# GpSimd's long instructions wait for their turn on the port that they share with VectorE, in a kernel whose order is written out ahead

## Chip, cores, metric

One core of a Trainium2 chip. The metric is the device time of one execution in microseconds, the median of the runs. In the profile PE is TensorE, PEld its weight loads, DVE VectorE, ACT ScalarE, POOL GpSimd and SP SyncE, whose queue issues most of the transfers.

## The reference

128 graphs of 64 nodes with 256 features pass through four layers, each added to its input and then normalised (layer norm):

```python
# layer 0: a gated graph network, five steps l
m = h @ weight[l]; agg = A.T @ m          # A = (adj != 0), per graph
r = sigmoid(agg @ Wir + h @ Whr + b); z = sigmoid(agg @ Wiz + h @ Whz + b)
n = tanh(agg @ Win + b + r * (h @ Whn + b)); h = (1 - z) * n + z * h
# layer 1: y = silu(rmsnorm(((adj + eps*I) @ x) @ W1 + b1) * w) @ W2 + b2
# layer 2: y = expmap0(adj @ logmap0(x)), projected onto the unit ball
# layer 3: attention by exp(e_i + f_j + b) over the neighbours
```

All of it is float32.

## The kernel before

Two graphs make a block of 128 rows and four blocks a group: 16 groups of 512 rows. `group(g)` writes a group's work: `gated` for the five steps of layer 0 (tiles hT, agg, tA, tB, U, V, hnb, banks p_ga, p_gb, p_gc, p_hx, p_hy, p_ix, p_iy), then layer 1 (aggm, ts, hid, sqt, sqh, xb, banks p_ah, p_bh, p_ch, p_ox, p_oy), layers 2 and 3 (tan, hw, x3T, banks ps_sup, ps_a, ps_att). Matrix products are cut into halves and combined by sums, in the manner of Strassen and Winograd, so that seven products do for eight. The sums of inputs are VectorE additions of two SBUF tiles (`sums`, line 445 in the profile: tA, tB, ts, s). The last two groups use simpler forms, and the last one is cut into pieces.

Nothing is issued where it is written. `flow.op(engine, us, run, writes, reads, ...)` records an operation with a planner's estimate `us` of its time and, for transfers, `kb`, a size that the planner uses. Work of several groups is open at a time. A search that is no part of the kernel made the string `ORDER`: each sign names the engine, the group and the place of the operation that is issued next. `Flow.placed` decodes it and `Flow.issue` calls each operation; on an engine each instruction is ordered behind the one before (`BEHIND`, which costs no semaphore). Between engines only true data dependencies hold an instruction back. So each engine follows its own list, and how two engines' lists run beside each other is decided on the chip.

An operation carries `port` where it uses the SBUF port that VectorE and GpSimd share: all GpSimd operations (`pool`, `few`, `few_s`, `pool_sum`, `w2_less`), and on VectorE those with two SBUF inputs (`summing`, `times_state`) or copies and scalings within SBUF. Before the change only the search used this mark.

GpSimd's longer work, with the profile's mean of one: additions of 128x512 in layer 1 (sqt, line 448: 1.3 us), additions of 128x1024 for biases (xb, x_n, line 448: 2.4 us), powers of a few numbers for norms (rstd line 845, inv line 1260, few lines 1151, 1323, 1341, 1345: 1.0 to 1.7 us), and at the start the sums of weights (w_a, w_in line 536; w2f line 681: 0.5 to 1.4 us). Its short operations (few, mv, ve, lines 438 and 442) take 0.2 to 0.3 us.

Row and feature layouts are exchanged by VectorE transposes of 32x32 squares (tile t, line 888 and 1366) and four SBUF transfers per tile on SyncE's queue (`moved`, line 790: hr from t, and x3T from t).

Of the kernel before, what the change touches and what calls it, by code (L numbers as in the profile page):

```python
# [53 lines left out]
class Flow:  # L54

    ENGINES, AHEAD = ("PE", "DVE", "ACT", "POOL", "SP"), 6
    SIGNS = "ABCDEFGHIJKLMNOPQRSTUVWXYZabcdefghijklmnopqrstuvwxyz0123456789!#$%&()*+,-./:;<=>"
    ORDER = ("CEEg~PhD~BNhED~BOiDC~Bs$CAAAAAAAAAAAAAAAAii~Nr~Nr~BO~N.~CU8~B+88~Bt~Bt8$~Bt~BL~Bt88li~BL~FU~FU~FU~FU"
             "~BL!i~Et~BL~Bt!~FZ~Bs~BL~FZ~BpEe~Bt~D%~BL~EO~BLA~DAi~DAB~DA~BoB~Bo~CUBF~BogiFFF~B+~B+HG~B+~GiAA~BK8~"
             "GjEC%~DB%B~BO%~FZAB~C3~BL~Es~E:~B<EA%B~CUlB~Et~BsB~CZBE~C5AB~CaE~BV~B+~C0~DiF,FA~D$H$~CBA~DE~CW~BsA~"  # L60
             "EQA$~BM~EQC&Ag~Dx~DBC~CV~DK~GK~Bs~CVgF&&~DxC~DGF%H~BsfBEF9(~EdA~B:AEj(jBB~Dx~D8~D8~MDAA~CJjkEBjFk~Mh"
             "x(~DA~Np~DAAx~MD~MDGl~BKT~NL~CJAH~DB~BdEA>CBAxe~Bdh~MBC~Lze~BpC~B+~Br!~BNxTA8TCG8~CB~CB~BN8B~J9!9DAD"
             "eAgDACCFB~CXCAAhBh~D8AKA~DABKK~DKKL~By~Do~BNLhFF~BV~BV#K~CAH#~G#PKhP~DA~Ce~B0~DA~Bt~DBKD~CAK~B0~BtPM"
             "~CAA~BV~By~IVA,P+CB8uh~BKA8A~Bp~Bq+gAC~BN~BNF;~BN~FZ~BNFBFBFuD~D%HFD~BQFKDGK~DjM~DF~Bu~BtL~Bt~Bt&M~B"
             "tMFHpFHFk%Fko&ooGoFqFGlopA(GpAlpH~BQA~BygG~CyoC&Ao&CoC~BQhAqGAG8Ag~BrBKGDKMA*DKgnKCh~DFnMDAPJBAKRDfK"
             "BD+B+B+~Bt~BQ~BQ~BQB+~JjEE~EP~D%E~BvpE~I3BK~BQB~BoA~DA~BqAA~BKA~B+~BoC~BM9~CUAA~BV~BVAAACBBC~Bo~Bo~B"
             "Veee!AC9FC~GAf~GAB8~CVABeGAg~EoC~Eo~BL~Bo(~BpA(AAAAB~CyAAKBKKAL!~BtA!kAA~BtCFCFBFFBFHFfHGKAAB~FeBKgK"
             "&CKkGKBMKKBKLBKK-~CA~CAKLM~ByM~ByMK~BU-KM~Bz~ByLK~BU~BVLKpKMKFBMFBKKBKMBKKBKK~BLEKE~BL~Ce~BL~Ce~Eo~C"
             "eEGEGLlL~DA~DA,,FKGKHKL~Bo~BoA~BqAAAG-~BoGC~BoK-9AG~BMAAGCAGAAB!88GC8ACBeeBgAfAC8B8B8BAGAGAC~Eo~BQJC"
             "*~EonA~BQ~BLAJA~BQAABAAAABAA~BMA!AfCACFF9FFBFHeBFfAFBFAgFBHFCKFBFBKqKGMFBHF~B:~B:H,~DALHo~B:L~B:~B:G"  # L70
             "F~BRp~CaKH~B;KFpH~BPBFBM~Bt~BtB%%LFBMBjlj~Bol~Buij~BLij~BL~BP~BLijEG%GL%jj~D8L~BQ~Cy~Bo&~DAFL~BR~H+L"
             "~BRF~H+L~BqF~BLHAALAA~B+~CBC~Bo~BqL~BMA~CUALAC~BVOA~BVAOB8ABsCeOB8CeGAgAfCB~GAF~GA8BA~CVAB~E+CA~BpjC"
             "kAA88AAABA~HUjBF~Bo!9A!AAlAHFGgeCGKKBKKKBMKfAGABFBg+G~CACK~BWBooBKBKM~Ce~BLoKB-~By~Byp~By~B0L~By~CeB"
             "q~CeMKB~HUMBKK~BziFE~BzFp~BUE~BL~BUE~EoL-oGop~Boq~CAp~CA~BL~CyGK~BLlK~BzM~Bo~BLFKG~DeHK~BLAAG~DAAG~B"
             "-A8CG~BoKG~BM8GAAG8CeAGfeBeeeeBg~BuACAgf8C8B~GAB~GAB8~B,AGAA~BQnC~Eo~BQJC~EoLAJ~BLAJ~BpAAABAAAABAA!A"
             "!FeCFFFCFHBF%BFfAABFBEgFGFCjBj(FB~B:~B:~B:BF~BtB(~Bt~Bt~BvGBjHAKHABAAoo~BpKBKLAAAAKG~BW~B:FBMB~BtBM~"
             "G%H~Bu~G%MFDG~BP~BMLF!~BQKgKGkHFCF~CaGFH~EtLDDHKLF~BQKDLCFK9gLFLCFqFDGFKFLFMFGAAFL~BRAACL(FALAALA8CL"
             "AeBA~D8BC8L8f~DAgpAA~CULCF~BVs~DKlAOBHA~BVsFG~BoOABAk~DKGABj~BV~By!kFg~ByFGDl~DKG~BV~DKAH~BVB~DK~DK~"
             "B0KGKK~B0KGC~By~CekM~ByC~CA,D+,~ByC~By~BU~B0B+~BWG~BV&KKMD~By~By~By~By~BWL8KqMAAGKGpCpAKCAAGK~BQAM*B"
             "LAJ~E:BK~BQKgAJ~BQJABCD~Bt~Bt~D%DC~CZ~IZDC~IZ~BQK~BQFFDFFK~CZH%~BvLFAAAAFBDFHFFGAA(AA~C3BH~BP~BPH~BP"  # L80
             "B~BPFlfKKB%~G%Gg+9j!B+KCBoHo~F*~FJ~E7~E7B!KK&gFLA!AA&ACAGKGCFApA-KGA~Bp-AjpqjBMAAlKBAF~Bu~EtLH~BtpA~"
             "Bt~BLoL~BtpFBKF~BL%LFfq~B:kKFL~BtfMA~D8~D8G~D8AAL(AAAL(AAApAFLAF,AAA9AAfFFL~ByfAHLAHAL~B+~B+~B+~B+~B"
             "Q~BY~B+A~BV~BysA~BKGs~CejkO~D+~BVA&AA~BVAAf~I8G~CefFB~BMF!~IeGGl~DKA~BVAH~FAK~BV~Ey~Ey~BQ~EyK~C!AGK~"
             "CeGK~CC~ByMkAAAG~BWAKG~JK~BU~CfK~CfKK,M~HyGo~BzoL-oKGqKMLnK~BQAnKMB~BdKLgK~BdKM~BQTK~BQCKT~BVKDLx!K>"
             "K!~CenCK~BzxCKLDKJDKD-T~BtK-~EPqKhhM~Bt~ErphoL~CZD~CZLh!~DFDpgDK~BQ~E:~BQFFgLKC~BaDFD~GjqDLF;DM~DjDD"
             "~B:D~FZHL~Bt~Bv~C3L~C3~BRF~Ca~E$~Bt~BP~E$~CaF~E$~CaCFDGDF~B:&DDCjGgjLgjAC~BQjLe~BRLeA~BML%g%Gg~CBjC~"
             "EPp~BRDFFL(FsDDFks~FA~BV~EyslF~BVHO~CZCG%~B:D&FDD&DF~BPGFDDF&(BF(~By9j~E$fH~ByBHKK~B0G~FAKKDG~EU~BM~"
             "Ce~BVFk!~D+~BVM~D++GC+C~CAl~C9F~C9KJ~BUGDK~C9HK~C9K~BWG~IeMDDKp~IALoLqoGM~BU~BUCGoCpogoGKqGGKMKCKKMB"
             "~Bt~BtoBKD~BVEKLEK~BuKEELFFFFFFKk~BWKKG-KGKMGKMIlp~E3(,P~C%LHoLp~C%PHKLPKII~CUqLPO~CUM~BoI~BRuAL~BKl"
             "eHL~CjpeHA!LFFCfIFFgfgeCe9CA~B,HABBBFRF999FF~BLBFHfjFB~E:H>~E:DgGKTKKFG!T%CGL%TFCFLl~D%D~BzH~D%D%~C5"  # L90
             "G%DFB!FkCKPGCKPPPlEGAAgF~CUBMD~CUFC~EUFGAAGCDGKCKIBMAA~BU+pC(H-AfADB~C8~C8KApoppAgDgDpKC~ByLH~DK~DK~"
             "CBCDKM~IACLK+L+DHMKL~GoKAAA,,A+pB+-ID~CfKLKM~By~ByLIAAAA~B,9IKKlBHH+HKK~CefFBFF9IBFHFFFF~CAFFH~BMBH!"
             "FGFG~D%G~D%%~BV%GCFF~Bqk~CZCL~CZ!%G%CBKFFkCKKGKf(~BtBl~BV~Bt~BuKFIMFMLoHAAMf9AAAAHALeHeeILA~BtHpK~BL"
             "MKGIAALLFFqfAAMAAf%HALAAALFFLAALeA~FALAA9AALA~DKfA~DKp~ByLeAAAf/A~DoG/~Bo~BoGs~Bo~BoFBO(AA~BVl888~BV"
             "AAIABFB~IeH~ByIHAAA~BzA~BMAIA~Bz!AABKHxK~EU~BVK~B7CKI~Do~Bd~DoLC~Do~By~B7~CgKD,T~BMK~C9K!>o~C9MTK~Cf"
             "FCTpFFLFoGKpMI~HyMCLoKpFF~CfhMFFkKDD&KlKKMDKD!KM~Ey#kklK~EyG~BUKKHDDhDK~C1DG~CBHKKkLHDDDDKDDHGKlKL!K"
             "GKGMKoM~DFpFqL~C3MLHFpFFKLKqL~Bt~Bt~BtG~Bt~BtM~Bt~BtFLFLFFLLL~By~By!~CeLp~DoDDDCDC~CeFL!8~B;C~DK/Asg"
             "sC~CZeOA~CZgCCkkkFFFCFF~BVF~BV~BVGkDFFFFFkFkF~B0F~CZ~CZDD~Ba~BV~CZ~DK~BV~DKGCF~DK~B0~BVD~DKDDDD~BV~D"
             "KKK;~B0KKM~By~By~By~ByKD9Bf~BWKMB~Ce~CeD~BMK,,oKL!KCKKCpKMDMKDMD~FAM~FA!LKKCBC+KK~C8BB~BOLKK,DKK$EL-"
             "EKKpKqKF~Bt,MLFoM~BP~BPL~BPpKKL~BPFFFLqk~BoMG~BoF~BRL88L(8L!~BM!L8LAAC~Fs~ByCFCLF~E$FFCFFCpFLAeOG/l~"  # L100
             "BVA~EyAOH~BVfO~C8BBIl~ByBYBl9~DPfYB~EZ~Ce~BEBl~DPBHfmBIDxC~BV~D:x~DKgI~IA~IA~BVKCKTK~BVKC~ByLIT~ByID"
             "~C8~Bil,D2KH,KYlDKILYgmKIY~BUm!LK~COKgLoLoCKI,IM~B$EKKDFDHGD~GjDkKKFML~DKk~DKD~CfKDKD;KKgFDM;DFDDk+g"
             "f+H,~C8~C8!~C8,~C8K~BVK~Cg,K~DKGMKL~BU--~BU~Bzo~BzK~BzM~BUp~BU~BuML~BUB~F8-poo~CBKp~ByM~ByB~ByKKKKKL"
             "~By~ByLKp~BWKK-KKq%,MFLoFLFpHKKLFLqFFMG~C3~BV8~BPL~BP~B:,8,F~BMA!LA,gFCL~BPjjLDlFH~BY~Bu~EyD&~DKC/D~"
             "DKGs~By~BV~ByOlGjH~DKGDDkDFDFGG~IADD~IAH~BV~BVK~BVKK~BVK~ByHM~ByG~BW~C8G+K~BW+kBKGKMpKLoooKG~BWKM~BV"
             "~BtM~G+KMLp+pGk~F8+KKqfM~EyGB~Bt*~CZKB*LD~BMKJ~BVJK~BQCKCKKKCKL~D%~BQ~Dj~BQDDL-DfKpKKK~BQ-~CZ~BQFMFF"
             "FKC~Bt~BtH9C~BQCFj,~B:MBj~BRFLEjHFiLo&i~BtDGEKpHjjLHjKGq~BtkFlL~BPH~G%G~GjMFG%G%LFlLF~BuH~EtL~Et~BV~"
             "BtA~BQ~Bt~Bu~BtLFLF%LFFkAG~B:CAC~BzF(~BzF~BzA(LFFOCAHs~BKHeOGCAOG9eCkACffFfCfACB~ByBFGAlJG~ByBBH~CeB"
             "f~CeB~DKG>K~B0KKTGK~ByMD~Do,~Dok~ByxCT~DKKkCok~BW~CeoCGKCK~BuMD~C8DK-L+~BW+Dq~ByLCF~BVFoMF~BVFMFFF,F"
             "KCG+Ck+CKG~E3EB~E:DG~BM~E:GCF~Et~B;KCk~C8CDKK~BuKH~Byp~EtDMF~BuDKKfCF~EPfFCDjFAGAAACFF~BVFA~BVAAGAF~"  # L110
             "BVCFAeAB(B(ACBFBAAAACAFClAAAHB8ABAGgAgAGkFCDAGC8FlD8GKC~BLK+CD~ByL~BoHBA~BWKGAGKC8GMAfAKB+KGg~CAKLgD"
             "~By~ByL-~ByA&MDA~BWKB~BUM~CeGMKg~Bz~HyC+~BzKLD~BUL~BU~BUGo-KGDKM*~EyM~ByLJ~EUJ~BzKLAJA~BVAA~BQ~BUKB~"
             "BQKDKKLK~Bt~BQLAAAA~EPB-~EPK~Bp~BvK-~EP~BQf~Bt~BvKBKKM9~D%MB~D%~Bv~CZL~CZ~DFLFFLFCFBKHK~BQCL%L%gF&FB"
             "qKHFLAGFM~BP~BPHLFHFLFH%G~GjH%gG~GFACG%G~F3CLFFBg~CUFHfAAHBFCA~BQA8AfAFLFF~BpAfAAAfAFfAAAGAAALAAeLFF"
             "pFeLeFGOAFOf~BRFfFs(~BVAAOAHkFHBAAA&AABAAGAAGeAAAA~BVBjF~BVkGAAAAlF~E7~FJB~E7~ByGA!AAHAAAA!GA~By~CnB"
             "KKGCTKK+CGx~CAMxD~BQ+g>~ByG+g>GKCxKGCKT~CAGMD~CAD~CAD~CA-LJ~CA~CCKJLq~C8~BtLJo~CBM~CB~CeJD~BUDD!K~Ba"
# [1326 lines left out]
```

## Time and profile before

| | |
|---|---|
| median of 3 runs | 2286.3 us (2285.16 to 2289.82) |
| the profiled execution: time, span | 2287.12 us, 2284.7 us |
| TensorE, weight loads, VectorE busy | 98%, 87%, 80% |
| ScalarE, GpSimd busy | 57%, 23% |
| granted TensorE clock | 0.994 |
| chain that ended last: TensorE, VectorE, DMA | 92%, 4%, 2% |

Busy time of TensorE is counted from the start to the modelled end of each matmul. Matmuls overlap, so a busy TensorE may still issue them more slowly than it could; the distance from one start to the next tells that. Every float32 matmul appears as two records. A duration on VectorE or GpSimd includes the time in which the instruction was blocked after its start.

### The profile page before, as it was taken

Reading aid. Unit: us, or ns where it says so; the run is one execution under the profiler, and the core shown is the slowest. Engines: PE = TensorE matmul, PEld = TensorE weight load, DVE = VectorE, ACT = ScalarE, POOL = GpSimd, SP = SyncE. Lnnn points to the kernel's source line nnn. Section 1 sums busy time; section 2 is a strip of 40 time slices with the busy share of each in tenths; the row PEclk is TensorE's granted clock in tenths of the full one; section 3 lists DMA queues with packets and bytes.
Section 4 is the critical chain, followed back from the end, with each engine's and each line's share of the span. In section 5 each row is a group of like instructions: output and inputs, shape, how many; then the busy total and the mean of one; then the engine's idle time right before and its main releaser. Section 6 shows DMA issues by size and latency. Waiting matters only on the chain.

```text
span 2284.7 us, 34183 instructions
## 1 busy us (share of the span) xinstructions
PE 2239.7 (98%) x12050; PEld 1983.1 (87%) x12050; DVE 1827.2 (80%) x3846; ACT 1304.0 (57%) x2842; POOL 533.6 (23%) x827
## 2 busy tenths in 40 slices
PE   8999999999999999999999999999999999999987
PEld 6888898888888898988989889898988989888875
DVE  6687788887887878888778887888788788877886
ACT  2444556665555656556565656656566565654565
POOL 4100213332213212132231212222122231210222
PEclk9999999999999999999999999999999999999998
DMA  5022112112212122121212212112221212211100
GB/s 155 15 29 37 22 28 59 19 22 47 56 15 45 37 31 56 22 40 28 35 40 36 51 22 39 39 29 47 31 37 29 40 38 35 42 29 19 33 20 28
DMA packets 430042, 84.58 MB, mean 37 GB/s; under 512 B 399236, under 2 KB 428960, under 8 KB 429872
## 3 DMA queue, kind: packets, MB, share of 16 engines
q1 hardware_dynamic: 428144, 80.52, 19.8%
q8 instruction: 95, 1.56, 0.3%
q10 hardware_dynamic: 1328, 1.31, 0.2%
q0 software_dynamic: 400, 0.57, 0.1%
q14 instruction: 75, 0.61, 0.1%
HBM read 32.55 MB, written 8.39 MB: 18 GB/s over the span
## 4 chain that ended last, share of the span: by engine, by line
PE 92%; DVE 4%; DMA 2%; SPq 1%; ACT 1%; issue 1%; POOL 0%; POOLq 0%; DVEq 0%; ACTq 0%
PE p_ga L926 23%; PE p_gc L926 11%; PE ps_agg L399 7%; PE p_ix L932 6%; PE p_hx L932 6%; PE p_gb L926 6%; PE p_ah L1109 5%; PE p_iy L932 4%; PE p_ox L1184 4%; PE p_hy L932 4%; PE p_oy L1184 3%; PE p_ch L1109 2%; PE ps_a L399 2%; PE ps_wmih L399 1%; PE ps_sup L399 1%; DMA hr<-t 1%
## 5 line engine op out<-in xcount | busy, mean ns | idle before, releaser
L442 POOL TENSOR_SCALAR mv<-st 128x4 f32<-128x4 f32 x56 | 16.3, 292 | 767.5 <-ACT x_n L828 422.6
L926 PE MATMUL p_ga<-hT,w_h 128*128 128x256 f32 x640 | 177.7, 380 | 1.1 <-DVE hT L1051 1.0
L926 PE MATMUL p_gc<-tA,w_h 128*128 128x256 f32 x640 | 178.5, 380 | 0.1
L926 PE MATMUL p_ga<-tA,w_h 128*128 128x256 f32 x640 | 177.7, 381 | 0.0
L926 PE MATMUL p_gc<-tB,w_a 128*128 128x256 f32 x640 | 175.7, 380 | 0.7 <-DVE tB L445 0.7
L926 PE MATMUL p_ga<-agg,w_a 128*128 128x256 f32 x640 | 173.3, 380 | 0.3 <-DVE agg L426 0.3
L926 PE MATMUL p_ga<-tB,w_a 128*128 128x256 f32 x640 | 171.8, 379 | 0.0
L399 PEld LDWEIGHTS ps_agg<-edge,hr 128*128 128x128 f32 x1024 | 148.3, 191 | 17.4 <-issue 2.8
L399 PE MATMUL ps_agg<-edge,hr 128*128 128x128 f32 x1024 | 152.4, 276 | 3.2 <-DMA hr<-t 3.2
L979 ACT ACTIVATE U<-U,half_b 128x512 f32<-128x512 f32 (+1 forms) x160 | 95.1, 629 | 91.2 <-DVE U L976 91.2
L430 ACT ACTIVATE hnb<-p_hx,half_b 128x256 f32<-128x256 f32 x197 | 92.6, 471 | 92.0 <-PE p_hx L932 74.5
L926 PEld LDWEIGHTS p_ga<-tB,w_a 128*128 128x128 f32 x640 | 120.3, 190 | 16.4 <-DVE tB L445 0.3
L926 PEld LDWEIGHTS p_gc<-tB,w_a 128*128 128x128 f32 x640 | 119.7, 190 | 17.0 <-DVE tB L445 1.3
L926 PEld LDWEIGHTS p_gc<-tA,w_h 128*128 128x128 f32 x640 | 118.7, 190 | 16.0 <-DVE U L992 0.5
L926 PEld LDWEIGHTS p_ga<-agg,w_a 128*128 128x128 f32 x640 | 118.2, 190 | 16.1 <-DVE agg L426 1.2
L926 PEld LDWEIGHTS p_ga<-hT,w_h 128*128 128x128 f32 x640 | 117.2, 190 | 16.1 <-DVE hT L1051 1.2
L926 PEld LDWEIGHTS p_ga<-tA,w_h 128*128 128x128 f32 x640 | 116.8, 191 | 15.8 <-ACT U L425 1.5
L979 ACT ACTIVATE V<-V,half_b 128x256 f32<-128x256 f32 (+1 forms) x160 | 89.1, 587 | 69.2 <-DVE V L976 68.7
L845 POOL TENSOR_TENSOR rstd<-ve,pow 128x4 f32<-128x4 f32 (+2 forms) x67 | 79.8, 1191 | 137.0 <-DVE ve L843 128.3
L992 DVE TENSOR_TENSOR V<-p_ix,V 128x256 f32<-128x256 f32 x192 | 80.6, 421 | 34.6 <-PE p_ix L932 30.3
L425 ACT COPY agg<-ps_agg 128x512 f32<-128x512 f32 x131 | 76.2, 583 | 47.2 <-PE ps_agg L399 45.8
L1184 PE MATMUL p_oy<-w2f,hid 128*128 128x128 f32 x720 | 101.1, 278 | 0.5 <-ACT hid L1160 0.4
(289 smaller groups left out, 6152.5 us busy)
## 6 DMA issues: line engine op xcount, KB each, us to landing
hr<-t SPq DMA_DIRECT2D x256, 128.0 KB, 3.8
x<-in_x_dram SPq DMA_DIRECT2D x64, 128.0 KB, 2.6
xr<-in_x_dram SPq DMA_DIRECT2D x16, 512.0 KB, 3.4
xs<-in_x_dram SPq DMA_DIRECT2D x120, 64.0 KB, 2.4
out_dram<-x_n SPq DMA_DIRECT2D x15, 512.0 KB, 2.9
x3T<-t SPq DMA_DIRECT2D x56, 128.0 KB, 3.8
edge<-in_adj_dram SPq DMA_DIRECT2D x64, 32.0 KB, 2.3
wm<-in_L_gnn_weight_dram SPq DMA_DIRECT2D x5, 256.0 KB, 3.8
```

The source lines that it names most:

```text
L399: return nc.tensor.matmul(o, lhsT, rhs, start=(k == 0), stop=(k == nk - 1))
L425: flow.either([("ACT", on_act(n, r), lambda: nc.scalar.copy(o(), i())), ("DVE", 0.145 + 0.00105 * n, lambda: nc.vector.tensor_copy(o(), i( ...
L430: flow.either([("ACT", on_act(n, r) if in_bank(r) else on_act(n + 108, r), lambda: nc.scalar.activation(o(), i(), AF.Identity, bias=bias() ...
L442: pool(0.23, lambda: nc.gpsimd.tensor_scalar(w[0](), x(), s0, s1, op0, *((op1,) if op1 else ())), [w[1]], r)
L845: pool(0.41 + 0.625 * m, lambda: nc.gpsimd.tensor_tensor(rstd[:, :m, :], ve[:, :m, :], pow2[:, :m, :NB], OP.pow), [rstd], [ve])
L926: pe(HR, lambda i=i, w=w, c=c: nc.tensor.matmul(ps[:, c * HR:(c + 1) * HR], w[:, m, c * P:(c + 1) * P], v[i][0](), start=first and i == 1 ...
L932: pe(HR, lambda: nc.tensor.matmul(ps[:, j * HR:(j + 1) * HR], w[:, m, :], v[0](), start=first, stop=True, skip_group_check=True), [ps], [( ...
L979: act(HR if len(w) == 1 else R, lambda: nc.scalar.activation(o(), src(), AF.Tanh, bias=half_b[:, i * KD + c:i * KD + c + 1], scale=0.5), w ...
L992: dve(HR + 6, lambda: nc.vector.tensor_add(uu[:, c, half(n)], region(ps, j), uu[:, c, half(n)]), [(uu, (n, c))], [ps, (uu, (n, c))])
L1109: pe(HR, lambda c=c: nc.tensor.matmul(ps[:, c * HR:(c + 1) * HR], w1f[:, w, (2 * q + c) * P:(2 * q + c + 1) * P], v[0](), start=first and ...
L1184: pe(128, lambda j=j, k=k: nc.tensor.matmul(ps[:, i * HR + j * P:i * HR + (j + 1) * P], val(v[k // 2])[:, k % 2, j * P:(j + 1) * P], w2f[: ...
```

## The change

`Flow.issue` remembers the last VectorE operation with `port` that it issued. A GpSimd operation with `port` and a planned time over 0.4 us is given a semaphore dependency on it: it starts once that VectorE instruction is done. The shorter GpSimd operations are given none, nor is VectorE ever made to wait for GpSimd. Some estimates are changed: TensorE's per width, the issue time of the four transfers of `moved` (0.6 to 0.7), and the `kb` of three kinds of transfers, which has no effect on the transfers themselves. `ORDER` is a new string throughout.

Both kernels issue the same number of instructions on TensorE (6210 matmuls), GpSimd and SyncE. An operation that may go to ScalarE or VectorE goes where its sign says: eight more are on VectorE and eight fewer on ScalarE, which has one more table load. GpSimd's waits on VectorE rise from 106 to 246.

```diff
 class Flow:
 
     ENGINES, AHEAD = ("PE", "DVE", "ACT", "POOL", "SP"), 6
+    LONG = 0.4
...
+    AFTER = mybir.DependencyInfo(mybir.DependencyClass.Sync, mybir.DependencyReason.DATA)
     BEHIND = mybir.DependencyInfo(mybir.DependencyClass.NoSync, mybir.DependencyReason.DATA)
...
     def issue(self):
-        last = {}
+        last, held = {}, None
         for eng, o in self.placed():
             made = o.ways[eng][1]()
+            if eng == "POOL" and eng in o.port and o.us > self.LONG and held is not None:
+                self.tc.add_manual_dep(made.ins, held.ins.name, self.AFTER, reason="the port in the plan's order")
             for i in made if isinstance(made, list) else [made]:
                 if eng in last:
                     self.tc.add_manual_dep(i.ins, last[eng].ins.name, self.BEHIND, reason="the plan's order")
                 last[eng] = i
+            if eng == "DVE" and eng in o.port:
+                held = last[eng]
...
     def pe(n, run, w, r):
-        flow.op("PE", {512: 0.863, 256: 0.433, 128: 0.219, 1: 0.2}.get(n, 0.3), run, w, r)
+        flow.op("PE", {512: 0.86, 256: 0.432, 128: 0.223, 1: 0.223}.get(n, 0.3), run, w, r)
...
-                    [(xs, (c, q))], kb=16 * n)
+                    [(xs, (c, q))], kb=36 * n)
...
-                edge[s][m::Q, :n, quads[t]], adj_blocks[t, (m % 2) * W:(m % 2 + 1) * W, blocks_in(g), :]), [(edge[s], m)], kb=8 * n)
+                edge[s][m::Q, :n, quads[t]], adj_blocks[t, (m % 2) * W:(m % 2 + 1) * W, blocks_in(g), :]), [(edge[s], m)], kb=14 * n)
...
-                flow.op("SP", 0.6, lambda q=q: nc.sync.dma_start(
-                    view(dst.tile())[:, q], t[W * q:W * (q + 1)].rearrange("r m x d -> r m (x d)")), [(dst, ("q", q))], [t], kb=32 * NB)
+                flow.op("SP", 0.7, lambda q=q: nc.sync.dma_start(
+                    view(dst.tile())[:, q], t[W * q:W * (q + 1)].rearrange("r m x d -> r m (x d)")), [(dst, ("q", q))], [t], kb=70 * NB)
```

## The prediction

> **What bounds the kernel now.** I read the page's shares first, then TensorE's time by matmul record, then the chain of waits, then the timeline at the chain's odd pieces. The page:
>
> ```profile
> span 2284.7 us, 34183 instructions
> ...
> PE 2239.7 (98%) x12050; PEld 1983.1 (87%) x12050; DVE 1827.2 (80%) x3846; ACT 1304.0 (57%) x2842; POOL 533.6 (23%) x827
> ```
>
> TensorE is the bound, and it computes the same 6210 matmuls after the change, so only its idle time can move. Busy time overlaps, so I took the distances between starts of successive matmul records in the trace. Packed, a 128x256 record takes 216 ns and a 128x128 one 112 ns. Everything over such a floor is lost: 63.6 us, plus 2.6 us before the first matmul and 9.2 us after the last. By stretch: 12.2 us in 0 to 100, 20.8 in 100 to 2100, 8.1 in 2100 to 2200, 22.6 in 2200 to 2275. The last is the final group's serial end; the written order there is nearly the same before and after, so I leave it and the 9.2 us alone. The rest has causes that the chain of waits (start, us, what) shows among its longest pieces:
>
> ```profile
> 480.14 4.10 DMA hr<-t
> ...
> 557.26 3.66 DMA hr<-t
> ...
> 1018.91 2.77 DVE hT L1051
> ...
> 1444.11 2.06 DVE few L1397
> ...
> 1556.01 2.47 DVE tA L445
> ...
> 1838.36 2.47 DVE tB L445
> ...
> 1977.80 2.51 DVE tB L445
> ...
> 2190.60 2.72 DVE hT L1051
> ...
> 2207.55 2.30 DVE few L854
> ```
>
> Seven single VectorE instructions of over 2 us lie on a chain that is otherwise matmuls. By tile, their usual length is another (ns, min/median/max):
>
> ```profile
> L445 DVE TENSOR_TENSOR tB<-tB,agg x80: 382/421/2579, 27.9 to 2170.0; 128x256 f32<-128x256 f32 x80
> ```
>
> and the timeline at 1838 us shows why:
>
> ```profile
> 1838.19 2.36 POOL L448 TENSOR_TENSOR x_n<-x_n,wb_r 128x1024 f32<-128x1024 f32 x1 [5.33 <-DVE t L1366]
> ...
> 1838.36 2.47 DVE L445 TENSOR_TENSOR tB<-tB,agg 128x256 f32<-128x256 f32 x1
> ...
> 1842.21 0.44 PE L782 MATMUL ps_hr<-ident,hT 128*128 128x128 f32 x2 [0.88 <-DVE hT L1051]
> ```
>
> GpSimd's addition began 0.17 us earlier; the 0.42 us subtraction ended only with it. Everything in VectorE's queue moved by 2 us, and TensorE lost 1.04 us waiting for hT.
>
> **What the Trainium skill says.** "SBUF — State Buffer", section "SBUF: two separate sides": VectorE with two SBUF inputs and GpSimd share a port pair as an exclusive lock for a whole instruction; whichever starts first blocks the other. The lines above agree. "GPSIMD Engine Reference", section "Elementwise — side-by-side cycle accounting", gives 4497 ns for an addition of 2048 elements; here 1024 elements take 2.36 us and 512 take 1.27, in proportion. "TensorE: Matmul & The Clock Gate", Part 1, says an idle TensorE falls to half clock for some microseconds; the trace agrees: behind the 2.4 us stall at 26.6 us the matmul records stand 0.42 us apart until 30.3.
>
> **The change part by part.**
>
> *The wait.* 307 GpSimd instructions are planned over 0.4 us. I laid the written order of before beside its trace: 89 of them started before the VectorE port instruction written ahead of them had ended, ahead by 145.8 us in all, at most 7.8. Against usual durations, 45 VectorE instructions ran at least 0.15 us too long, 42.1 us in all, each beside a GpSimd instruction under way. Following each into TensorE's losses:
> - Head: four w2f subtractions from 24.8 us on lengthen w_in, tA, tB and w_a; TensorE stalls 2.41 us (p_hx<-tA) and 1.33 us (p_hx<-hT), and the half clock behind adds 1.83. Sum 5.6.
> - Middle, a loss after each collision at 450, 773, 1019, 1173, 1444, 1556, 1838 and 1978 us: 0.50 + 0.61 + 0.80 + 0.55 + 0.66 + 0.99 + 1.04 + 0.89 = 6.0.
> - Last groups: at 2190.6 (hT behind x_n) 2.11 + 0.37, at 2207.6 (few behind xb) 1.80. Sum 4.3.
>
> Together 15.9 us, 38% of the 42.1; the other collisions were hidden behind queued matmuls. The wait removes the case where GpSimd jumps ahead. It does not stop VectorE's next port instruction from running into a GpSimd one: in the new order the next such instruction is written close enough for that behind 138 of the 307 (141 before). Those are foreseen, so I count 80% of 15.9: **-12.7 us**; the ends are 0 and -15.9.
>
> *What the wait costs.* GpSimd's waits on VectorE go from 106 to 246, in 105 added wait instructions; the nearest row, VectorE's own EVENT_SEMAPHORE at line 445, has 21 ns in the median, so some 2 us on an engine busy for 23%: nothing on the path. What counts is lateness. Behind a held instruction stand GpSimd's tiny ones (mv, ve, few, 0.2 to 0.3 us), and ScalarE's x_n waits for those: the waits view has
>
> ```profile
> ACT x_n L833 <- POOL mv L442: 33.0, 22, 6.1
> ```
>
> TensorE itself waits for a GpSimd result only once past its first matmul, 1.4 us at ps_rms (2230). For the long additions the cover is large: x_n had 11.9 to 18.6 us until its reader in the collisions above, xb 10.7 to 18.6. If that cover were gone, the cost is the slower rival's. I take 0 here, between 0 and +24 us (derived there).
>
> *Order and planner numbers.* The costs given to the planner don't run; their effect is the order. TensorE's waits between 100 and 2100 us (total, times, longest) begin with late transfers:
>
> ```profile
> PE ps_agg L399 <- DMA hr<-t: 2.7, 4, 0.9
> PE ps_a L399 <- DMA x3T<-t: 1.6, 2, 0.9
> PE ps_hr L782 <- DVE hT L1051: 1.5, 2, 0.9
> ```
>
> In start distances that is 1.11 + 1.03 + 0.81 + 0.38 + 0.63 for hr and 0.93 + 1.04 for x3T: 5.9 us. One such issue occupies SyncE for 0.68 us in the median, and the planner reckoned 0.6; now it reckons 0.7 and a heavier transfer, so work goes ahead of readers of hr. All 617 SyncE transfers remain; so do POOL's. Half of 5.9: **-3.0 us**, ends 0 and -5.9. Eight copies or scalings more on VectorE and eight fewer on ScalarE (0.4 to 0.6 us each) and one more table load (1.28 us) lie on engines busy 80% and 57%, under TensorE; if uncovered, at most 5 us. A new order also has slips of its own, as before had (474, 485, 2182 to 2187 us: some 4.5 us with no collision): **+3.0**, ends 0 and +6.
>
> Sum: -12.7 - 3.0 + 3.0 = -12.7 us. The profiled execution took 2287.1 us (span 2284.7 and 2.4 around it), so 2274.4; the median of the runs lies 0.8 below that execution, hence **2273.5 us**.
>
> **The rivals.**
>
> *GpSimd becomes late (slower).* Of the 89 that ran ahead, 45 had a first reader closer than their lead, mostly the next GpSimd instruction in a chain of pow and few; held back, they would pass their readers by 63.7 us. If 38% of that reached TensorE, as with the blocked VectorE time, it is +24.2 against -15.7: 2294.8 us. It decides from 25% on (15.7/63.7). Against it: the order was made with those starts counted late, and TensorE hardly waits for GpSimd today. For it: normalisation chains run POOL, ScalarE, POOL in series.
>
> *The collisions stay (no change).* GpSimd starts just as the VectorE instruction it waited for ends, and the next one runs into it. The 138 close neighbours speak for it, the lengths of the leads (up to 7.8 us) against. Then only the transfers' part less the slips is left: about 2286 us.
>
> *All of it goes.* The full 15.9 and 5.9 vanish and the new slips stay near 2: 2287.1 - 19.8 - 0.8 gives about 2266; without slips 2264.
>
> **How the numbers follow.** My forecast (2269 to 2280) 0.60; all gone (2262 to 2269) 0.14; collisions stay (2280 to 2289) 0.15; slower (2289 to 2300) 0.11. The range 2264 to 2289 leaves out the slower rival and the extreme of the best case. A measurement can tell 0.2%, 4.6 us: faster means below 2281.7, which takes the first two and a little of the third, 0.76; within 0.2% 0.13; slower 0.11.
>
> **What would show it.** Right: tB<-tB,agg, tA<-tA,hT and hT<-hT,V at a maximum well under 2 us outside the head; no DVE piece over 2 us in the middle of the chain; no 2.4 us stall at 26 us; fewer waits on hr; more GpSimd idle time ended by VectorE, with the same 1.27 and 2.36 us per addition. Wrong: TensorE waiting for ps_rms, x_n or tan in the middle (slower rival); as many stretched VectorE instructions as before (no change); a stall in the middle that the plan left.

## Result and the profile after

| | before | after |
|---|---|---|
| median of four runs (lowest to highest) | 2287.02 us (2285.16 to 2289.82) | 2267.28 us (2265.47 to 2268.51) |
| the profiled execution: time, span | 2287.12 us, 2284.7 us | 2266.71 us, 2264.3 us |
| ratio of the times, 95% interval | | 0.9912 (0.9895 to 0.9929) |

The kernel is 19.7 us faster, where 12.7 had been forecast. The page of the kernel after, its head and its first part:

```profile
span 2264.3 us, 34277 instructions
...
PE 2232.2 (99%) x12050; PEld 1983.9 (88%) x12050; DVE 1807.8 (80%) x3854; ACT 1303.4 (58%) x2835; POOL 523.2 (23%) x827
```

VectorE has eight instructions more and GpSimd the same, yet they are busy for 19.4 and 10.4 us less: blocked time counts as busy time, and that is what shrank (VectorE's by 27.0 us, below). By the chain that ended last (shares of the span), VectorE's part falls from 4% to 2% and TensorE's rises from 92% to 95%:

```profile
PE 95%; DVE 2%; ACT 1%; DMA 1%; SPq 0%; issue 0%; POOL 0%; POOLq 0%; DVEq 0%; ACTq 0%
```

Of the chain's pieces between 100 and 2100 us the four of 4 us and more (start, us, what) are transfers; a single VectorE instruction of over 2 us is no longer among its pieces there:

```profile
472.65 4.03 DMA hr<-t
507.01 4.16 DMA hr<-t
1546.61 5.23 DMA x3T<-t
1688.68 4.15 DMA x3T<-t
```

The subtraction that ran 2.58 us before is at most 1.5 us long now (ns: min/median/max; 454 is the line that was 445):

```profile
L454 DVE TENSOR_TENSOR tB<-tB,agg x80: 382/420/1509, 21.7 to 2154.2; 128x256 f32<-128x256 f32 x80
```

The timeline of the kernel after shows the wait at work on an x_n addition:

```profile
363.50 0.65 DVE L992 SCALAR_TENSOR_TENSOR V<-V,hnb 128x512 f32<-128x512 f32 x1
364.07 0.74 DVE L1077 SCALAR_TENSOR_TENSOR ea<-ident,eps_c,adjT 128x512 f32<-128x512 f32 x1
364.38 2.65 POOL L457 TENSOR_TENSOR x_n<-x_n,wb_r 128x1024 f32<-128x1024 f32 x1 [6.75 <-DVE V L992]
```

GpSimd stood idle for 6.75 us until V, its turn in the order, was done. It then met ea, already under way, and was the one to be lengthened: 2.65 us instead of 2.36. No loss of TensorE over 0.3 us follows before 466 us.

This ea reads SBUF alone but does not carry the mark `port`, so the mark does not cover every VectorE instruction that can be blocked, and no wait is ever tied to ea. Its collision with an xb is the longest that is left, 2.08 us instead of 0.74:

```profile
2122.20 2.37 POOL L457 TENSOR_TENSOR xb<-x_n,b_r 128x1024 f32<-128x1024 f32 x1 [0.61 <-ACT x_n L439]
...
2123.04 2.08 DVE L1077 SCALAR_TENSOR_TENSOR ea<-ident,eps_c,adjT 128x512 f32<-128x512 f32 x1
```

I laid the written order beside this trace as I had done for the kernel before. None of the 307 long GpSimd instructions starts ahead of its turn (89 before). VectorE instructions that run at least 0.15 us too long are 27, with 15.1 us in all, the longest by 1.3 us (45 with 42.1 us before). All 27 are written behind the GpSimd instruction that they run into. Before, some 32 of the 42.1 us belonged to 27 instructions that are written ahead of it. So the wait removed all of the jumps ahead, and what is left is the other kind of collision, which the prediction said it would not stop. Losses of TensorE over its floors, in the stretches of the profiled executions:

| us | before | after | e1: old order, wait | e2: new order, no wait |
|---|---|---|---|---|
| 0 to 100 | 12.2 | 5.4 | 8.7 | 11.5 |
| 100 to 2100 | 20.8 | 13.0 | 12.5 | 23.1 |
| from 2100 to the last matmul | 30.7 | 25.0 | 26.8 | 28.1 |
| sum | 63.6 | 43.4 | 48.1 | 62.7 |

The drop of 20.2 us is the span's, 20.4, within the rounding. The stretch before the first matmul (2.6) and behind the last (9.1) are as they were. One trace carries an uncertainty: three kernels with the same beginning (before, e3 and e5) lose 12.2, 13.8 and 13.6 us in their first 100. And the profiled execution of e2 took 2285.1 us, 3.1 more than that kernel's median, so its column stands for one of its slower executions.

GpSimd now idles for VectorE where it did not before; two of its waits (us in total, times, longest):

```profile
POOL sqt L457 <- DVE tA L454: 55.5, 12, 11.3
POOL few L1332 <- DVE tB L454: 54.5, 4, 15.8
```

Its additions keep their lengths, 1.28 us in the mean for sqt and 2.36 for xb.

What TensorE waits for between 100 and 2100 us, the first four lines:

```profile
PE ps_a L408 <- DMA x3T<-t: 1.4, 2, 1.0
PE p_hy L941 <- DVE hT L1060: 1.1, 1, 1.1
PE ps_sup L408 <- ACT tan L1314: 1.0, 2, 0.7
PE ps_agg L408 <- DMA hr<-t: 0.9, 2, 0.7
```

And ScalarE's wait for GpSimd's short instructions, where lateness would have shown first; it was 33.0 us with a longest of 6.1:

```profile
ACT x_n L842 <- POOL mv L451: 28.9, 22, 4.4
```

### The profile page after: what moved, and what is told of

It reads as the page before. It is cut to its first block, busy times and chain, and to the rows that moved or that the text cites. A ratio compares the mean times of both kernels' runs of the same rounds, so it can differ in the third digit from the quotient of the medians.

```text
span 2264.3 us, 34277 instructions
## 1 busy us (share of the span) xinstructions
PE 2232.2 (99%) x12050; PEld 1983.9 (88%) x12050; DVE 1807.8 (80%) x3854; ACT 1303.4 (58%) x2835; POOL 523.2 (23%) x827
## 3 DMA queue, kind: packets, MB, share of 16 engines
q8 instruction: 95, 1.56, 0.3%
## 4 chain that ended last, share of the span: by engine, by line
PE 95%; DVE 2%; ACT 1%; DMA 1%; SPq 0%; issue 0%; POOL 0%; POOLq 0%; DVEq 0%; ACTq 0%
PE p_ga L935 24%; PE p_gc L935 12%; PE ps_agg L408 7%; PE p_ix L941 6%; PE p_hx L941 6%; PE p_gb L935 6%; PE p_ah L1118 5%; PE p_ox L1193 5%; PE p_iy L941 5%; PE p_hy L941 4%; PE p_oy L1193 3%; PE p_ch L1118 2%; PE ps_a L408 2%; PE p_bh L1118 1%; PE ps_att L408 1%; PE ps_wmih L408 1%
## 5 line engine op out<-in xcount | busy, mean ns | idle before, releaser
L451 POOL TENSOR_SCALAR mv<-st 128x4 f32<-128x4 f32 x56 | 17.6, 315 | 744.6 <-ACT x_n L837 425.0
L935 PEld LDWEIGHTS p_ga<-hT,w_h 128*128 128x128 f32 x640 | 117.4, 191 | 14.4 <-issue 0.5
```

The costliest lines, as they stand in the source:

```text
L451: pool(0.23, lambda: nc.gpsimd.tensor_scalar(w[0](), x(), s0, s1, op0, *((op1,) if op1 else ())), [w[1]], r)
L935: pe(HR, lambda i=i, w=w, c=c: nc.tensor.matmul(ps[:, c * HR:(c + 1) * HR], w[:, m, c * P:(c + 1) * P], v[i][0](), start=first and i == 1 ...
```

## The experiments

The expectations name theories by letters. A: the collisions on the port that reached TensorE are what the wait took away. Against it stand the new order by itself, and lateness of GpSimd as a cost. Three groups of kernels were timed, each beside runs of the kernel before (medians 2285.49, 2286.4 and 2286.9 us). Times are medians; all ratios are to the kernel before. e4 is the kernel after without some of its waits and turned out equal to it, so within the first group it stands for the kernel after.

**e1: the old order with the wait.** `ORDER` and the planner's numbers of before, the wait of the change:

```diff
-        last = {}
+        last, held = {}, None
...
+            if eng == "POOL" and eng in o.port and o.us > self.LONG and held is not None:
+                self.tc.add_manual_dep(made.ins, held.ins.name, self.AFTER, reason="the port in the plan's order")
...
+            if eng == "DVE" and eng in o.port:
+                held = last[eng]
```

> The order and the planner's numbers of before, with the wait added: 307 long GpSimd operations wait for the VectorE port operation written ahead of them. Theory A (the jumps ahead were the loss, the wait stops them): 12 to 16 us less than before, ratio 0.993 to 0.995, blocked VectorE time from 42 us to under 20. Theory B (the new order with its heavier transfers does it, the wait is beside the point): within 3 us of before. Theory C (held GpSimd becomes late): slower than before.

2271.31 us, ratio 0.994 (0.9926 to 0.9953): -14.2 us, with bounds of -16.9 and -10.7. Nothing but the wait differs. Blocked VectorE time falls to 14.4 us in 25 instructions, and the subtraction of tB is at its plain length everywhere:

```profile
L451 DVE TENSOR_TENSOR tB<-tB,agg x80: 381/418/427, 26.4 to 2158.1; 128x256 f32<-128x256 f32 x80
```

What TensorE waits for in the middle of e1, all that is listed:

```profile
PE ps_agg L405 <- DMA hr<-t: 2.1, 3, 1.0
PE ps_a L405 <- DMA x3T<-t: 1.6, 2, 1.1
PE p_ga L932 <- DVE hT L1057: 1.0, 1, 1.0
PE p_hx L938 <- ACT hnb L436: 0.8, 1, 0.8
PE p_hx L938 <- DVE hnb L437: 0.2, 1, 0.2
```

The waits of before behind collisions (V, tB, y, ts) are gone. The transfers are nearly as late as before (2.7 and 1.6): the wait does not touch them.

**e2: the new order without the wait.** The kernel after with

```diff
-    LONG = 0.4
+    LONG = 99.0
```

> The new order without any of the added waits. Theory A: GpSimd jumps ahead again, blocked VectorE time again near 40 us; 3 to 8 us less than before (transfers, slips), so 2279 to 2284 us. Theory B: as fast as after, 2267 us. Theory C: faster than after.

2282.01 us, ratio 0.9989 (0.9981 to 0.9997): -3.5 us by the medians. Blocked VectorE time is 48.3 us in 51 instructions, so this order collides somewhat more than the old one where nothing holds GpSimd. From e2 to e4 is -14.8 us, the wait's worth in the new order; -14.2 was its worth in the old. The order is worth -3.5 without the wait, by medians (-2.5 by the ratio, with bounds of -4.3 and -0.7), and -4.1 (e1 to e4) with it. As far as these runs can tell, the two parts add. The order's part includes the eight operations that moved from ScalarE to VectorE, which were not tried by themselves.

One place tells it in a pair. The timeline of e2 at the start, where four w2f subtractions run as soon as their transfer has landed:

```profile
24.82 5.69 POOL L690 TENSOR_TENSOR w2f<-w2f 128x512 f32<-128x512 f32 x4 [18.01 <-DMA w2f<-in_L_gnn_W_dram]
25.06 1.57 DVE L454 TENSOR_TENSOR tA<-hT 128x512 f32<-128x512 f32 x1
26.56 1.49 DVE L545 TENSOR_TENSOR w_a<-w_a 128x256 f32<-128x256 f32 x1
27.97 3.22 DVE L545 TENSOR_TENSOR w_in<-w_in 128x128 f32<-128x128 f32 x4
...
31.84 1.95 PE L408 MATMUL ps_wmih<-wihT,wmT 128*128 128x512 f32 x2 [3.19 <-DVE wmT L651]
```

and the same place in the kernel after:

```profile
25.16 1.14 DVE L545 TENSOR_TENSOR w_in<-w_in 128x128 f32<-128x128 f32 x4
...
26.39 5.64 POOL L690 TENSOR_TENSOR w2f<-w2f 128x512 f32<-128x512 f32 x4 [19.59 <-DVE w_in L545]
...
27.56 1.02 PE L408 MATMUL ps_wmih<-wihT,wmT 128*128 128x512 f32 x2
```

With the wait, w2f starts 1.6 us later, the four w_in subtractions take 1.14 us instead of 3.22, and TensorE's wait of 3.19 us for wmT does not occur. Behind that wait e2's two matmuls of ps_wmih also take 1.95 us where the kernel after has 1.02, the half clock of which the prediction spoke: the granted clock is 0.5 from 32.0 to 35.4 us in e2, and 1.0 from 6 us to 2207 us in the kernel after.

**e3: the wait for the wide additions alone.** e1 with `LONG = 2.0`, which leaves only xb and x_n (128x1024, 30 instructions) waiting.

> The order of before, the wait only on the 30 additions of 128x1024 (xb, x_n). By theory A the collisions of these alone go: 0.80 + 0.55 + 0.66 + 0.99 + 1.04 + 0.89 in the middle, 2.48 + 1.80 in the last groups, 9.2 us, so 2277 to 2280 us (ratio 0.996). Theory B: no change. If the collisions with the 1.3 us additions (sqt) matter as much as those with the 2.4 us ones, 3 us or less.

2276.55 us, ratio 0.9962 (0.9949 to 0.9975): -8.9 us; blocked VectorE time 27.2 us in 39. A tenth of the long instructions brings more than half of what the wait brings.

**e4: the new order, no wait on powers.** The kernel after with

```diff
+POWERS = (1.04, 1.66, 0.41 + 0.625, 0.41 + 0.625 * 2)
...
+        self.power = self.eng == "POOL" and self.us in POWERS
...
-            if eng == "POOL" and eng in o.port and o.us > self.LONG and held is not None:
+            if eng == "POOL" and eng in o.port and o.us > self.LONG and not o.power and held is not None:
```

> The kernel after, with the wait taken from the 128 powers (rstd, inv, few), kept on the additions. In the traces no VectorE port instruction that started during a power was stretched (0 of 38 before, 0 of 22 after). If powers don't block VectorE, nothing is lost: the same as after within 2 us, or up to 4 us less if their lateness cost something (theory C in part). If the port lock covers powers too, 3 us or more above after.

2267.24 us, ratio 0.9924 (0.9912 to 0.9937). That is the kernel after's time, with the same 15.1 us of blocked VectorE time in 27 instructions. The condition takes the wait from all 142 powers (the expectations here and for e5 say 128, a miscount). Their waits do nothing that shows, good or bad.

**e5: the old order, wait on powers alone.** e1 with `and o.power` in the condition.

> The order of before, the wait only on the 128 powers. They don't block VectorE (0 of 38), so there is nothing to gain and what is measured is the price of lateness alone: in the trace of before, 29 of the 89 operations that ran ahead are powers, ahead by 35.3 us. Theory A: no change, within 3 us of before. Theory C (late GpSimd reaches TensorE at 38%): about 10 us or more above before.

2287.89 us, ratio 1.0006 (0.9998 to 1.0014): +1.5 us by the medians, which the interval does not tell from none. Blocked VectorE time 41.9 us in 44 instructions, as before, and tB is stretched as before:

```profile
L455 DVE TENSOR_TENSOR tB<-tB,agg x80: 382/419/2576, 27.2 to 2171.3; 128x256 f32<-128x256 f32 x80
```

**e6: every GpSimd operation waits for the last VectorE operation of any kind.** The kernel after with

```diff
-            if eng == "POOL" and eng in o.port and o.us > self.LONG and held is not None:
+            if eng == "POOL" and eng in o.port and held is not None:
...
-            if eng == "DVE" and eng in o.port:
+            if eng == "DVE":
```

> The kernel after, but every GpSimd operation that has the port mark, long or short, waits, and for the last VectorE operation of any kind written ahead of it: more waits and later ones. Theory A (what is planned late is late without harm): within 3 us of after, 2265 to 2270 us. Theory C: each short operation on the chain of a norm now waits up to 0.7 us more, 8 us or more above after.

2296.83 us, ratio 1.0041 (1.0027 to 1.0055): 29.5 us over the kernel after. I had put the harm at no more than 3 us under theory A, and that missed: a wait can be late enough to cost more than the collisions did. The middle loses 34.1 us and the end 33.3 (13.0 and 25.0 in the kernel after). Two edits were made at once here, so e9 and e10 make each by itself.

**e7: the wait at the start alone.** e1 with `and o.stream == 0` in the condition, which is the sums of weights.

> The order of before, the wait only on the weight sums of the start (w2f, w_a, w_in). Theory A: the head's 5.6 us go (2.41 + 1.33 of stalls, 1.83 of half clock), so 2279 to 2282 us, ratio 0.9975; no stall of over 2 us at 26 us. If the head's stall has another cause (a transfer, the weights), no change.

2282.2 us, ratio 0.9982 (0.9975 to 0.999): -4.2 us (bounds of -5.7 and -2.3), where 5.6 had been expected. The stall at 33 us is gone, and so is the half clock behind the one at 26 us, which is shorter, 1.56 instead of 2.41 us. By the prediction's own terms that is 0.85 + 1.33 + 1.83 = 4.0. The rest of the stall stays: its tA sums stand behind three w_in subtractions in VectorE's own list, which no wait on GpSimd changes.

**e8: the wait in both directions.** The kernel after, and VectorE's port instructions wait for the last long GpSimd addition written ahead of them:

```diff
+            if eng == "DVE" and eng in o.port and long is not None:
+                self.tc.add_manual_dep((made[0] if isinstance(made, list) else made).ins, long.ins.name, self.AFTER, reason="the port in the plan's order")
+            if eng == "POOL" and eng in o.port and o.us > self.LONG and o.us not in POWERS:
+                long = made
```

> The kernel after, where in addition VectorE's port operations wait for the last long GpSimd addition written ahead of them. The stretched VectorE time (15 us after) turns into waiting of the same length, and VectorE loses the right to go first when GpSimd is late. Theory A: no gain, from the same as after to 10 us slower. If the rest of the collisions were still costing time by jumps of VectorE, up to 3 us faster.

2266.75 us, ratio 0.9914 (0.9901 to 0.9928), the time of the kernel after. Blocked VectorE time is 2.4 us in 3 instructions: VectorE's idle time that GpSimd ends has grown from 7.9 to 27.3 us instead. What was blocking at the port has become waiting for a semaphore, and the time is the same.

**e9: short GpSimd operations wait too.** The first edit of e6 alone.

> The kernel after with the limit of 0.4 us gone: the short GpSimd operations wait as well, for the same VectorE port operation written ahead. It splits the 29.5 us that the run with every wait lost against after. If the harm comes from short operations being held at all (they stand in the chains of the norms), most of it, 15 us or more, is here: 2282 us or more. If it comes from waiting for VectorE operations that don't use the port, this is within 5 us of after.

2268.15 us, ratio 0.992 (0.9906 to 0.9933): 0.9 us over the kernel after, which these runs do not tell from nothing. Waits of the short instructions by themselves are not the harm of e6.

**e10: long operations wait for any VectorE operation.** The second edit of e6 alone.

> The kernel after, where the long GpSimd operations wait for the last VectorE operation of any kind written ahead, not the last one with the port mark; short ones don't wait. If the harm comes from short operations being held, this is within 5 us of after. If it comes from waiting for VectorE operations that don't use the port, many of which read PSUM behind TensorE, it is 15 us or more above: 2282 us or more.

2289.12 us, ratio 1.001 (1.0003 to 1.0016): 21.8 us over the kernel after. So this edit is most of the harm, though it does two things at once: GpSimd waits for another kind of instruction, and for one that is written later. The two were not separated. The two edits of e6 together cost 6.8 us more than 0.9 and 21.8. The largest single loss, first by e10's waits of TensorE from 2100 us, then by its timeline:

```profile
PE ps_o L408 <- POOL w2f L690: 4.7, 1, 4.7
```

```profile
2237.34 0.18 DVE L851 BATCH_NORM_AGGREGATE mv<-st 128x2 f32<-128x6 f32 x1
2237.75 0.17 DVE L851 BATCH_NORM_AGGREGATE mv<-st 128x2 f32<-128x6 f32 x1
2238.05 1.26 POOL L690 TENSOR_TENSOR w2f<-w2f 128x512 f32<-128x512 f32 x1 [8.98 <-DVE mv L851]
...
2239.37 1.76 PEld L408 LDWEIGHTS ps_o<-w2f,hid 128*128 128x128 f32 x8 [4.84 <-POOL w2f L690]
```

The last w2f subtraction is held for 8.98 us by an mv that has no part in the port, and TensorE stands for w2f. In the middle TensorE waits for GpSimd directly, which it never does in the kernel after:

```profile
PE ps_ss L408 <- POOL sqt L457: 2.6, 3, 1.2
PE ps_rms L1163 <- POOL few L1160: 1.3, 1, 1.3
```

Behind one of these waits, at 408 us, the granted clock is 0.5 for 3.4 us, which costs 1.7 us more. The rest is spread. ScalarE's x_n waits for GpSimd's few grow from 12.1 us in 14 times to

```profile
ACT x_n L439 <- POOL few L447: 38.0, 33, 3.9
```

while 27.4 us of VectorE time are still blocked. I did not follow the other parts of the 22 us to their places.

## Why the prediction was right, and by how much it was off

**What bounds the kernel, and by what.** Right. Only TensorE's idle time moved, and it moved by the span's difference.

**The collisions: 15.9 us, counted at 80%.** The mechanism was right. The wait alone took 14.2 us from the old order (e1; the interval also holds the 12.7 forecast and the whole 15.9) and 14.8 from the new one (e2 to e4). That the size came out close is partly luck. The bill was too short: behind the collision at 2190 us the granted clock was 0.5 from 2194.2 to 2197.6 us, as it was behind the one at 26 us, and the matmul records of that stretch lost 1.7 us more, which the prediction left out. In e1 and in the kernel after the clock is not lowered in either place. (The length of a stall alone does not tell: one of 1.56 us in e1 left the clock at 1.0, and behind one of 1.40 us in e10, at 408 us, it fell to 0.5.) So the bill was 17.6 us and not 15.9.

The fifth taken off stood for the 138 places where VectorE's next port instruction is written close behind. Such collisions do remain, 27 of them, but in the trace after no loss of TensorE over 0.3 us between 100 and 2100 us stands within 4 us behind one. They are short, 0.56 us on average against 0.94 before. What e1 did not get back lay elsewhere: at the start 3.5 us came of 5.6, since 1.56 us of the stall at 26 us stay (e7), and from 2100 us on 3.9 came of 6.0, where e1 has a new wait of 1.36 us for an x3T at 2185 us. In the middle the whole of the 6.0 went.

**Which additions.** The start is worth -4.2 (e7), the wide additions -8.9 (e3), the powers nothing that can be told from none (e5: +1.5). If the parts add, that leaves 1.1 to 2.6 of e1's 14.2 for the 98 additions of 128x512, less than the intervals of e1 and e3 can resolve. The prediction had priced these at 0.50 + 0.61 = 1.1 (450 and 773 us). This share follows by subtraction and was not measured by itself.

**The start, 5.6 us.** Put down wholly to the collisions, it belonged to both parts. In the traces the wait alone brings the first 100 us from 12.2 to 8.7; the new order with the wait brings them to 5.4, and without it only to 11.5 (e2). So at the start each part is worth more with the other, though one trace is uncertain by some 1.6 us there. In VectorE's list of the kernel before the tA sums come behind the w_in subtractions (e7), and the prediction did not price that the order changes this: in the list of the kernel after they come ahead, from 18.1 us on.

**The order: -3.0 for transfers, +3.0 for new slips, net 0.** This is the step that failed, and most of the difference of 7.0 us lies here: the order brought -3.5 to -4.1 (e2, e1 to e4). By stretches, from e1 to the kernel after: -3.3 at the start, +0.5 in the middle, -1.8 at the end. So the two terms did cancel in the middle, for which they were worked out, but each at about half its size. In start distances, hr and x3T cost 3.9 us there, where e1 has 4.4 and before had 5.3. (The 5.9 of the prediction includes one of 0.63 at 2158 us, so -2.1 of the -3.0 forecast came. Of the 3.9, 0.81 us at 553 us stand under tA in the waits, where hr and tA came at almost the same time.) Slips without a collision come to 3.9 us (466 to 477, 1396 and 1525 us: the waits for hT and tan shown above among them), where e1 has 2.6 (470, 481 and 1139 us). The prediction had added 3.0 for new slips without taking off the old order's own, which go with it; the net in the middle was +1.3. What was missing was the start, and the stretch behind 2100 us, where in e1 an x3T still costs 1.36 us at 2185 and under 0.3 in the kernel after.

The rest of the 7.0 us between forecast and result is 1.5 us for the wait (14.2 instead of 12.7) and about 1.5 us that the medians of the kernel before differ by, 2287.02 beside the kernel after and 2285.49 beside e1, e2 and e4.

**The wait's lateness, taken as 0.** Right for this wait: the powers and their chains, on which the slower rival was built, wait without any effect (e4), and ScalarE's waits for GpSimd add up to 60.0 us before and 61.9 after. One of the prediction's signs of being wrong did come, TensorE waiting for tan in the middle, 1.0 us in 2 times. But e2, where nothing is held, has the same two waits with the same 1.0 us, so they belong to the order. The price of +24 was not absurd, though. With another VectorE instruction to wait for, lateness costs 22 us (e10), and 29.5 with the short operations waiting as well (e6). What protects the change is the choice of what is waited for: the last instruction that carries the mark `port`, not the last of any kind.

**The signs and the rivals.** The longest tB<-tB,agg is 1.51 us and the longest tA<-tA,hT 0.64, as forecast. hT<-hT,V still reaches 1.78 us, which is hardly "well under 2". Slower: not with this wait. The collisions stay: no, 42.1 us of blocked time became 15.1. All of it goes, about 2266 us: nearest to the 2267.3 measured, and given 0.14. The range held the result, but the likeliest case, 2269 to 2280, did not.

**Left open.** The middle lost 8.3 us less in e1 than before, and the eight collisions that I had followed there explain 6.0 of it, the transfers 0.9; the other 1.4 us are spread over losses of under 0.25 us each and were not followed. Why the end of e10 and e6 is longer by some us, apart from w2f, was not followed either.

## What to carry to other kernels

Where two engines share a port and each follows its own list, let the engine with slack wait, and only for instructions that take the port: that was worth 14 us of 2286 in either order, while the same wait tied to the last VectorE instruction of any kind gave all of it back and more. In this kernel waits for GpSimd's short powers could be left out at no cost. Price such collisions from the trace by following each stretched instruction to the bounding engine's next gap; 42 us of stretched time held 17.6 us that counted, the half clock behind two of the stalls included, and 14 of these could be had. When an order is set anew, price its start and its end as well as its steady stretch, since a slip of the queue there has no queued work to hide it.

## What the runs showed of the hardware

GpSimd's powers take the port from nobody, though they have two SBUF inputs and last up to 1.7 us. The timeline of the kernel before:

```profile
970.52 1.67 POOL L845 TENSOR_TENSOR rstd<-ve,pow 128x8 f32<-128x8 f32 x1
970.77 0.65 DVE L445 TENSOR_TENSOR tA<-hT 128x512 f32<-128x512 f32 x1
971.45 0.43 DVE L445 TENSOR_TENSOR tA<-hT,tA 128x256 f32<-128x256 f32 x1
```

Two VectorE additions of two SBUF tiles start while the power runs and have their plain lengths. Of 38 VectorE port instructions that started during a power (at least 0.15 us before its end) none was stretched in the kernel before, and none of 22 in the kernel after. During a sqt addition it was 25 of 29, during xb and x_n 8 of 8. The Trainium skill ("SBUF — State Buffer", section "SBUF: two separate sides") has the pair locked for the whole of a GpSimd instruction. That agrees with the additions of 128x512 and 128x1024, not with these powers of 2 to 8 numbers in a row; there the measurement decides, and the times of e4 and e5 fit it. Whether it is the few columns or the long computing of each that leaves the port free was not tried.
